# Small triangular matrices turned round through DRAM in wide rows, both chunks and four heads side by side

## The chip, the cores and the metric

The kernel runs on one core of one Trainium2 chip. The metric is device time in microseconds (us). Lower is better.

## The reference

Six residual blocks on x of 1024 tokens by 256 channels: a gated feed-forward with ternary weights, windowed differential attention, the same feed-forward again, a feed-forward whose weights come from a table of 16 values, a gated delta rule, and the table feed-forward again. Only the delta rule bears on this change. It has 16 heads of 128 key and 128 value channels and a state S of 128x128 for each head:

```python
S = S * gt[..., None]
pred = einsum('bhk,bhkv->bhv', kt, S)
delta = (vt - pred) * bt[..., None]
S = S + kt[..., None] * delta[:, :, None, :]
o = einsum('bhk,bhkv->bhv', qt, S)
```

## The kernel before

All matrices are float32. x stays in SBUF, 8 tiles of 128 tokens. The blocks run one after the other; the delta rule (`delta_rule`, L509) takes the span from about 582 to 1706 us.

*The delta rule in chunks.* The 128 tokens of a tile are a chunk; the 16 heads are taken in 4 groups of 4 (HG). Two chunks of one head group are a pair; there are 16 pairs. In a chunk the recurrence becomes a triangular system: keys by keys, decayed, is a strictly lower triangle of 128x128 for each head, and the kernel needs the inverse Z of one plus this triangle, scaled. A pair has 2 chunks x 4 heads = 8 such triangles.

*How Z is made.* The diagonal 16x16 blocks of the triangles are inverted on VectorE (`solve`); the larger blocks are then filled in by matmuls, 16 to 32, 32 to 64, 64 to 128 (`invert`). VectorE wants all 64 diagonal blocks of a pair (8 triangles x 8 blocks) one per partition, with a block's 256 numbers along the partition's row. The matmuls leave the triangles with 64 columns and the row index over the partitions. To get from one layout to the other the data goes through DRAM and back, three times for each pair:

- *dm.* `triangle` (L769) fills the SBUF tile `ml` (128 partitions, 2 chunks, 4 heads, 64 columns) level by level (L850). It is written to the DRAM tile `dm` (L839), one of `[4, 129, 64]` for each chunk. `solve` (L875) reads the 16x16 blocks from there into `xb` (L884), one DMA for each chunk and head, and then multiplies `xb` with `diag` into `nb` (L895), where VectorE's inversion begins (L902 to L933).
- *z.* The inverted blocks `zb` are written block by block to a DRAM array of zeros (L945, one DMA for each chunk and head), and read back as rows (L950, two halves for each chunk).
- *zt.* The same with the transposed blocks `ztb` and full rows of 128 (L945, L947).

The helper `blocks` (L868) gives the 8 diagonal blocks of one triangle in DRAM as a hand-built access pattern: block step 16 x (pitch + 1), row step the pitch, then 16 numbers. The DRAM arrays for z and zt are filled with zeros once, at the start of the delta rule (L605 to L612); there are two sets, used by pairs in turn.

*A neighbour on the same queue.* `prepare` (L661) writes the 8 x 128 scaling coefficients `cf` to DRAM as `cfd` (L684), and `solve` reads them back as `diag` (L879) two pairs later:

```python
cfd = us[0]["cfd"] = dram.tile([2, HG, P], F32, name="cfd", bufs=4)
nc.sync.dma_start(out=cfd.rearrange("c h r -> r c h"), in_=cf)
```

*What sets the order.* Every DMA is issued by the sync engine (SP), in one queue. The pairs overlap: `weave` (L1107) mixes the steps of `prepare` for pair i+2, `triangle` for pair i+1, `solve`, `invert`, `values` and `gates` for pair i, and `advance` and `emit` (the recurrence itself and the output) for pair i-1, by fractions written out at L1141 to L1152. That is the order of the program. The framework then orders each engine's instructions by a simulated timeline (`schedule_with_timeline_sim=True`, L1253) and inserts the semaphore waits. On the chip each engine and the sync queue run strictly in the order so fixed.

Of the kernel before, what the change touches and what calls it, by code (L numbers as in the profile page):

```python
# [10 lines left out]
F32 = mybir.dt.float32  # L11
# [7 lines left out]
P = 128  # L19
# [16 lines left out]
BLK = 16  # L36
HG = 4
NG = NH // HG
NEG = -1e30


# [467 lines left out]
def delta_rule(tc, a, x, xnT, pp, bc, kon, ones, kdw, first):  # L509
# [22 lines left out]
    nc = tc.nc  # L532
# [10 lines left out]
    with ExitStack() as ctx:  # L543
# [49 lines left out]
        small = ctx.enter_context(tc.tile_pool(name="dsm", reuse_waits="tile", bufs=2))  # L593
        blk = ctx.enter_context(tc.tile_pool(name="dblk", reuse_waits="tile", bufs=1))

        turns = []
        for i in range(2):  # L600
            turn = {}
            for nm in ("ml", "mt16", "mt32"):
                turn[nm] = cst.tile([P, 2, HG, 64], F32, name=f"{nm}_{i}")
                nc.gpsimd.memset(turn[nm], 0.0)
            for nm in ("z", "zt"):  # L605
                turn[nm] = dram.tile([2, HG, P, P], F32, name=f"{nm}_{i}", bufs=1)
                for c in range(2):
                    for r in range(2):
                        nc.sync.dma_start(
                            out=turn[nm][c].rearrange("h r s -> r h s")[:, :, 64 * r : 64 * r + 64],  # L610
                            in_=turn["mt16"][:, c],
                        )  # L612
            turns.append(turn)

# [8 lines left out]
        mhalf = cst.tile([P, HG], F32, name="mhalf")  # L623
        nc.gpsimd.memset(mhalf, -0.5)

        lo, hi = slice(0, 64), slice(64, 128)

        parts = [(c, h, half) for c in range(2) for h in range(HG) for half in (lo, hi)]

# [139 lines left out]
        def triangle(us):  # L769

            p = us[0]["p"]
            k, kq, qk, d, turn = p["k"], p["kq"], p["qk"], p["d"], p["turn"]
            kf, d = (t.rearrange("p c h t -> p (c h t)") for t in (k, d))
            full = p["qkf"] = lev.tile([P, 2, HG, P], F32, name="qkf", bufs=3)
            nc.gpsimd.memset(full[hi, :, :, lo], 0.0)
            mt64 = p["mt64"] = lev.tile([64, 2, HG, 64], F32, name="mt64", bufs=2)  # L780
            for i, n in enumerate(LEVELS):
                runs = 64 // n
                rights = lambda ap: ap.rearrange("p b (s two l) -> p b s two l", two=2, l=n)[:, :, :, 1, :]
                if n < 64:
                    pm = pmm.tile([P, 2, 2 * HG, 32], F32, name="pm", tag="pm")
                    for c, h, half in parts:
                        nc.tensor.matmul(  # L787
                            pm[half, :, c * HG + h, :].rearrange("p b (s l) -> p b s l", l=n),
                            lhsT=k[:, c, h, half],
                            rhs=rights(kq[:, :, c, h, half]),  # L790
                            start=True,
                            stop=True,
                        )
                else:

                    pm = pmm.tile([P, 2, 2, HG // 2, 64], F32, name="pm6", tag="pm")
                    for c in range(2):
                        for h in range(HG):
                            nc.tensor.matmul(
                                pm[hi if h % 2 else lo, :, c, h // 2, :],  # L800
                                lhsT=k[:, c, h, lo],
                                rhs=kq[:, :, c, h, hi],
                                start=True,
                                stop=True,
                            )

                dl, dr = (d.rearrange("p (s two) -> p s two", two=2)[:, :, j] for j in range(2))
                kqr = kq.rearrange("p b c h (s two l) -> p b (c h s) two l", two=2, l=n)[:, :, :, 1, :]
                nc.vector.tensor_mul(  # L809
                    kqr,  # L810
                    kqr,
                    dl.unsqueeze(1).unsqueeze(3).to_broadcast([P, 2, 2 * HG * runs, n]),
                )
                kl = left(kf, n)
                nc.gpsimd.tensor_mul(kl, kl, dr.unsqueeze(2).to_broadcast([P, 2 * HG * runs, n]))  # L815
                d2 = lev.tile([P, 2 * HG * runs], F32, name=f"d{i}", bufs=3 if n == 64 else 1)
                nc.gpsimd.tensor_mul(d2, dl, dr)
                d = d2
                if n == 64:
                    for j, half in enumerate((lo, hi)):  # L820
                        nc.scalar.copy(mt64[:, :, j:HG:2, :], pm[half, 0])
                        nc.scalar.copy(full[lo, :, j:HG:2, hi], pm[half, 1])
                    yield
                    continue
                if n == 32:
                    for r0 in (0, 64):
                        at = slice(r0, r0 + 32)
                        nc.scalar.copy(
                            turn["mt32"][at, :, :, 32:64], pm[at, 0].rearrange("p (c h) t -> p c h t", c=2)
                        )  # L830
                        nc.scalar.copy(qk[at, :, 32:64], pm[at, 1])
                    for half in (lo, hi):
                        nc.scalar.copy(full[half, :, :, half], qk[half].rearrange("p (c h) t -> p c h t", c=2))
                    for c, u in enumerate(us):

                        dm = u["dm"] = dram.tile([HG, P + 1, 64], F32, name="dm", bufs=4)
                        for half in (lo, hi):
                            r0 = half.start + half.start // 64
                            nc.sync.dma_start(  # L839
                                out=dm[:, r0 : r0 + 64, :].rearrange("h r s -> r h s"), in_=turn["ml"][half, c]  # L840
                            )
                    yield
                    continue
                mask = kon[:, K_M + i * 32 : K_M + (i + 1) * 32]
                run4 = lambda ap: ap.rearrange("p h (s l) -> p h s l", l=n)
                pred4 = run4(all_heads(mask.bitcast(I32)))
                dst = lambda t: t.rearrange("p h (s two l) -> p h s two l", two=2, l=n)[:, :, :, 1, :]
                flat = lambda t: t.rearrange("p c h t -> p (c h) t")
                if n < BLK:
                    nc.vector.copy_predicated(dst(flat(turn["ml"])), pred4, run4(pm[:, 0]))  # L850
                else:
                    nc.vector.tensor_mul(dst(flat(turn["mt16"])), run4(pm[:, 0]), run4(all_heads(mask)))
                nc.vector.copy_predicated(dst(qk), pred4, run4(pm[:, 1]))
                yield
            p["dall"] = d
            kst = p["kst"] = lev.tile([P, 2, HG, P], F32, name="kst", bufs=2)
            for c, u in enumerate(us):
                if u["n"] < NT - 1:
                    pk = pmm.tile([P, HG, P], F32, name="pk", tag="pm")
                    for h in range(HG):  # L860
                        nc.tensor.transpose(pk[:, h, :], k[:, c, h, :], ident)
                    nc.scalar.copy(kst[:, c], pk)
                u.update(
                    qk=full[:, c], kt=kq[:, 0, c], qt=kq[:, 1, c], kst=kst[:, c], dall=d[:, c * HG : (c + 1) * HG]
                )
                yield

        def blocks(ap):  # L868

            pitch = ap.shape[-1]  # L870
            return bass.AP(
                tensor=ap.tensor, offset=ap.offset, ap=[[BLK * (pitch + 1), P // BLK], [pitch, BLK], [1, BLK]]
            )

        def solve(us, vb):  # L875


# [3 lines left out]
            for c, u in enumerate(us):  # L881
                for h in range(HG):
                    q0 = 32 * c + 8 * h
                    nc.sync.dma_start(  # L884
                        out=xb[q0 : q0 + 8].rearrange("b (i j) -> b i j", j=BLK),
                        in_=blocks(u["dm"][h]),
                    )
            yield
            mat = lambda t: t[:, 0:256].rearrange("p (r c) -> p r c", c=BLK)
# [47 lines left out]
            )  # L937
            z = us[0]["z2"] = lev.tile([P, 2, HG, 64], F32, name="z", bufs=1)
            zt = us[0]["zt2"] = lev.tile([P, 2, HG, P], F32, name="zt", bufs=2)
            for c, u in enumerate(us):  # L940
                for got, to in ((zb, "z"), (ztb, "zt")):
                    full = u["p"]["turn"][to][c]
                    for h in range(HG):
                        q0 = 32 * c + 8 * h
                        nc.sync.dma_start(out=blocks(full[h]), in_=got[q0 : q0 + 8])  # L945
                    if to == "zt":
                        nc.sync.dma_start(out=zt[:, c], in_=full.rearrange("h r s -> r h s"))  # L947
                        continue
                    for r in (slice(0, 64), slice(64, 128)):
                        nc.sync.dma_start(out=z[r, c], in_=full[:, r, r].rearrange("h r s -> r h s"))  # L950
            yield

        def invert(us):
# [303 lines left out]
```

## Time and profile before

| | |
|---|---|
| median of 3 runs | 1788.56 us (1786.34 to 1804.77) |
| the profiled execution | 1780.44 us, its span 1778.7 us |
| mean granted TensorE clock | 0.902 |
| the delta rule, 582 to 1706 us | PE busy 989 of 1124 us |
| its steady part, 770 to 1540 us | PE 706, DVE 579, ACT 478, POOL 328 of 770 us |
| zt read (L947), dm write (L839), z read (L950) | 32, 64, 64 issues of 256, 64, 64 KB |
| xb read (L884), z and zt writes (L945) | 128, 128, 128 issues of 8 KB |
| cfd write, diag read (L684, L879) | 16, 16 issues of 4 KB |

PE is TensorE, DVE VectorE, ACT ScalarE, POOL GpSimd, SP the sync engine; a q after the name is an engine's sequencer, which waits and issues but does not compute. Arrows in the profile point from what is read to what is written: dm<-ml is the DMA that writes dm from ml. In the views of waits a row gives who waited for whom, the total, the number of times and the longest. The packets of a DMA are the runs of bytes that are contiguous on both sides; the profile counts a DMA's semaphore updates as packets too.

### The profile page before, as it was taken

What the parts mean: (1) busy time and instruction counts of PE and PEld (TensorE: products, weight loads), DVE (VectorE), ACT (ScalarE), POOL (GpSimd) and SP (SyncE); (2) the same over time, 40 slices, a digit from 0 to 9 for tenths busy, and PEclk for the clock granted to TensorE, in tenths of its full rate; (3) what the DMA queues carried; (4) which work ended last, traced back from release to release, by engine and by line L of the source; (5) the groups of instructions that cost most, each with busy time, mean ns of one, the idle gap of its engine ahead of it and who ended that gap; (6) DMA issues with size and microseconds to landing.
All of it is one profiled execution on the core that took longest, in us unless ns stands there. A gap on an engine that the chain in (4) does not pass through costs nothing.

```text
span 1778.7 us, 33398 instructions
## 1 busy us (share of the span) xinstructions
PE 1528.3 (86%) x13136; PEld 1105.3 (62%) x13152; DVE 1181.4 (66%) x2567; ACT 879.9 (49%) x2019; POOL 535.5 (30%) x470
## 2 busy tenths in 40 slices
PE   7885868777999766899889889898999998998879
PEld 3433545545455445677767677777777776776745
DVE  3999976574232356767768678786778877877221
ACT  2116273735222344546736646764656674675321
POOL 0022323131001034434533344543434452543100
PEclk9998989889999866798989889999889998989889
DMA  7020000002002001031111121112121120111100
GB/s 243 32 54 26 4 19 1 1 1 66 1 0 44 4 1 30 9 54 28 23 15 40 20 54 28 20 19 46 35 45 24 22 48 9 38 26 20 60 1 24
DMA packets 150349, 54.94 MB, mean 31 GB/s; under 512 B 116784, under 2 KB 142704, under 8 KB 149936
## 3 DMA queue, kind: packets, MB, share of 16 engines
q1 hardware_dynamic: 150192, 52.81, 12.8%
q8 instruction: 104, 1.70, 0.4%
q14 instruction: 53, 0.43, 0.1%
HBM read 39.11 MB, written 11.70 MB: 29 GB/s over the span
## 4 chain that ended last, share of the span: by engine, by line
PE 45%; DVE 22%; ACT 15%; DMA 6%; issue 5%; POOL 3%; SPq 2%; another core or an unknown queue 0%; DVEq 0%; ACTq 0%; POOLq 0%
PE ps L638 6%; PE pg L135 4%; PE po L160 4%; PE pu L135 4%; DMA dm<-ml 4%; PE pm L787 3%; ACT e L319 3%; DVE kq L809 2%; PE pg L697 2%; PE po L365 2%; DVE other L195 2%; PE px L1097 2%; PE pss L675 2%; DVE k L652 2%; PE pr L253 2%
## 5 line engine op out<-in xcount | busy, mean ns | idle before, releaser
L815 POOL TENSOR_TENSOR k<-k,d 128x512 f32<-128x512 f32 x96 | 156.3, 1628 | 299.2 <-PE pm L787 193.3
L787 PE MATMUL pm<-kq,k 128*64 128x64 f32 x3072 | 134.3, 237 | 25.9 <-POOL kq L739 11.0
L787 PEld LDWEIGHTS pm<-kq,k 128*64 128x64 f32 x3072 | 114.6, 148 | 59.1 <-issue 35.7
L809 DVE TENSOR_TENSOR kq<-kq,d 128x1024 f32<-128x1024 f32 x96 | 129.6, 1351 | 23.1 <-remote 8.9
L319 ACT ACTIVATE e<-ps,nm 128x128 f32<-128x128 f32 x256 | 91.5, 397 | 63.6 <-DVE nm L314 62.3
L652 DVE SCALAR_TENSOR_TENSOR k<-ps,pp,k 128x256 f32<-128x256 f32 x192 | 84.9, 475 | 41.7 <-ACT k L650 40.4
L652 DVE SCALAR_TENSOR_TENSOR q<-ps,pp,q 128x256 f32<-128x256 f32 x192 | 86.5, 479 | 24.6 <-ACT q L650 21.7
L652 DVE SCALAR_TENSOR_TENSOR v<-ps,pp,v 128x256 f32<-128x256 f32 x192 | 87.5, 475 | 16.2 <-ACT v L650 14.7
L638 PE MATMUL ps<-xnT,wq 128*128 128x259 f32 x256 | 82.2, 458 | 0.0
L253 PE MATMUL pr<-xnT,wq 128*128 128x512 f32 x128 | 62.9, 625 | 20.8 <-DVE nm L314 9.3
L987 PE MATMUL dz<-zt,mz 64*64 64x32 f32 x1024 | 79.6, 231 | 0.2 <-issue 0.2
L979 PE MATMUL dz<-mz,zt 64*64 64x32 f32 x768 | 73.3, 228 | 7.1 <-ACT mz L972 7.1
L638 PE MATMUL ps<-xnT,wv 128*128 128x259 f32 x256 | 76.5, 425 | 1.2 <-DVE qk L733 0.6
L365 PE MATMUL po<-wo,oT 128*128 128x256 f32 x256 | 64.5, 396 | 14.2 <-ACT oT L362 12.9
L1097 PE MATMUL px<-wdo,oT 128*128 128x256 f32 x256 | 70.8, 422 | 6.6 <-ACT oT L1093 6.4
L650 ACT ACTIVATE q<-ps,pp 128x256 f32<-128x256 f32 x64 | 30.4, 475 | 92.3 <-PE ps L638 92.3
L739 POOL TENSOR_TENSOR kq<-q,ge 128x1024 f32<-128x1024 f32 x16 | 53.5, 3346 | 64.8 <-PE pso L1069 36.6
L987 PEld LDWEIGHTS dz<-zt,mz 64*64 64x64 f32 x1024 | 65.5, 144 | 11.9 <-issue 10.1
L638 PE MATMUL ps<-xnT,wk 128*128 128x259 f32 x256 | 71.6, 417 | 0.5 <-ACT k L650 0.5
L346 POOL TENSOR_TENSOR d<-d,dz 128x512 f32<-128x512 f32 x32 | 34.3, 1072 | 117.3 <-DVE dz L345 86.0
L964 PE MATMUL pmz<-z,mt 64*64 64x64 f32 x1024 | 56.5, 234 | 14.9 <-DMA z<-z 9.9
L964 PEld LDWEIGHTS pmz<-z,mt 64*64 64x64 f32 x1024 | 43.1, 141 | 41.9 <-issue 15.8
(213 smaller groups left out, 3985.9 us busy)
## 6 DMA issues: line engine op xcount, KB each, us to landing
zt<-zt SPq DMA_DIRECT2D x32, 256.0 KB
dm<-ml SPq DMA_DIRECT2D x64, 64.0 KB
z<-z SPq DMA_DIRECT2D x64, 64.0 KB
wq<-in_aWq SPq DMA_DIRECT2D x1, 2048.0 KB
wo<-in_aWo SPq DMA_DIRECT2D x1, 2048.0 KB
wk<-in_dWk SPq DMA_DIRECT2D x4, 512.0 KB
wq<-in_dWq SPq DMA_DIRECT2D x4, 512.0 KB
wv<-in_dWv SPq DMA_DIRECT2D x4, 512.0 KB
```

Source lines behind the costliest of these rows:

```text
L135: nc.tensor.matmul(ps[:n], lhsT=w[:, c, cs], rhs=xnT[:, c, cols], start=(c == 0), stop=(c == KC - 1))
L253: nc.tensor.matmul(pr, lhsT=w[:, c, hcol : hcol + HD], rhs=xnT[:, c, PAD + hf * 512 : PAD + (hf + 1) * 512], start=(c == 0), stop=(c == KC ...
L319: nc.scalar.activation(e[:, s, j, :], ps[:, s, j, :], AF.Exp, bias=nm[:, 4 * s + j : 4 * s + j + 1], scale=SUB**-0.5, accum_out=z[:, s, j ...
L365: nc.tensor.matmul(po, lhsT=oT[:, h, :], rhs=wpool["wo"][:, g * HG + h, :], start=(h == 0), stop=(h == HG - 1),)
L638: nc.tensor.matmul(ps[:, 0 : 2 * P + 3], lhsT=w[nm][:, c, h * HD : (h + 1) * HD], rhs=xnT[:, c, PAD + t0 - 3 : PAD + t0 + 2 * P], start=(c ...
L652: nc.vector.scalar_tensor_tensor(yh, xi, pp[:, col : col + 1], yh, ALU.mult, ALU.add)
L787: nc.tensor.matmul(pm[half, :, c * HG + h, :].rearrange("p b (s l) -> p b s l", l=n), lhsT=k[:, c, h, half], rhs=rights(kq[:, :, c, h, half]),
L809: nc.vector.tensor_mul(kqr, kqr, dl.unsqueeze(1).unsqueeze(3).to_broadcast([P, 2, 2 * HG * runs, n]),)
L815: nc.gpsimd.tensor_mul(kl, kl, dr.unsqueeze(2).to_broadcast([P, 2 * HG * runs, n]))
L964: nc.tensor.matmul(pmz[half, c, h], lhsT=p["turn"][f"mt{n}"][half, c, h], rhs=z[half, c, h], start=True, stop=True,)
L987: nc.tensor.matmul(runs(dz[half, 1, c, h]), lhsT=mz[half, c, h], rhs=right(zt[half, c, h, half], n), start=True, stop=True,)
L1097: nc.tensor.matmul(px, lhsT=oT[:, h, :], rhs=u["w"]["o"][:, h, :], start=(h == 0), stop=(h == HG - 1))
```

## The change

A pair's eight triangles are kept in one flat DRAM array in which a row holds both chunks and all four heads: 2 x 4 x 64 numbers, 2 KB (`ROW` = 512), for dm and z, and 2 x 4 x 128 numbers, 4 KB, for zt. So a row in DRAM has the same order as a partition's row in SBUF. Rows 64 to 127 of dm and z are shifted by 64 numbers (`rows`), so that one step of `blocks` still walks all eight diagonal blocks of a triangle. Its pitch is now the wide row, and triangle i begins at i x width.

```diff
+ROW = 2 * HG * 64
...
+        def rows(ap, half):
+            o = half.start * ROW + half.start
+            return ap[o : o + 64 * ROW].rearrange("(r s) -> r s", s=ROW)
+
+        def blocks(ap, i, width):
+            pitch = 2 * HG * width
+            return bass.AP(
+                tensor=ap.tensor,
+                offset=ap.offset + i * width,
+                ap=[[BLK * (pitch + 1), P // BLK], [pitch, BLK], [1, BLK]],
+            )
...
-                turn[nm] = dram.tile([2, HG, P, P], F32, name=f"{nm}_{i}", bufs=1)
-                for c in range(2):
-                    for r in range(2):
+                wide = ROW if nm == "z" else 2 * ROW
+                turn[nm] = dram.tile([P * wide + 64], F32, name=f"{nm}_{i}", bufs=1)
+                zero = turn["mt16"].rearrange("p c h t -> p (c h t)")
+                if nm == "z":
+                    for half in (lo, hi):
+                        nc.sync.dma_start(out=rows(turn[nm], half), in_=zero[half])
+                else:
+                    for j in range(2):
...
-                    for c, u in enumerate(us):
-                        dm = u["dm"] = dram.tile([HG, P + 1, 64], F32, name="dm", bufs=4)
-                        for half in (lo, hi):
-                            r0 = half.start + half.start // 64
-                            nc.sync.dma_start(
-                                out=dm[:, r0 : r0 + 64, :].rearrange("h r s -> r h s"), in_=turn["ml"][half, c]
-                            )
+                    dm = p["dm"] = dram.tile([P * ROW + 64], F32, name="dm", bufs=2)
+                    for half in (lo, hi):
+                        nc.sync.dma_start(
+                            out=rows(dm, half), in_=turn["ml"][half].rearrange("p c h t -> p (c h t)")
+                        )
...
-                        in_=blocks(u["dm"][h]),
+                        in_=blocks(u["p"]["dm"], c * HG + h, 64),
...
-            for c, u in enumerate(us):
-                for got, to in ((zb, "z"), (ztb, "zt")):
-                    full = u["p"]["turn"][to][c]
-                    for h in range(HG):
-                        q0 = 32 * c + 8 * h
-                        nc.sync.dma_start(out=blocks(full[h]), in_=got[q0 : q0 + 8])
-                    if to == "zt":
-                        nc.sync.dma_start(out=zt[:, c], in_=full.rearrange("h r s -> r h s"))
-                        continue
-                    for r in (slice(0, 64), slice(64, 128)):
-                        nc.sync.dma_start(out=z[r, c], in_=full[:, r, r].rearrange("h r s -> r h s"))
+            turn = us[0]["p"]["turn"]
+            for got, to, width in ((zb, "z", 64), (ztb, "zt", P)):
+                for i in range(2 * HG):
+                    nc.sync.dma_start(out=blocks(turn[to], i, width), in_=got[8 * i : 8 * i + 8])
+                if to == "zt":
+                    nc.sync.dma_start(
+                        out=zt.rearrange("p c h t -> p (c h t)"),
+                        in_=turn[to][0 : 2 * P * ROW].rearrange("(r s) -> r s", s=2 * ROW),
+                    )
+                    continue
+                for half in (lo, hi):
+                    nc.sync.dma_start(out=z[half].rearrange("p c h t -> p (c h t)"), in_=rows(turn[to], half))
```

For each pair the dm writes go from 4 DMAs of 64 KB to 2 of 128 KB, the z reads from 4 to 2, the zt reads from 2 to 1; the 8 block reads of dm and the 16 block writes of z and zt stay, each of 128 runs of 64 bytes. The block writes of z now stand for both chunks ahead of the z reads, then those of zt ahead of the zt read; before, chunk 0's z and zt stood ahead of chunk 1's. The zero fills go from 16 DMAs to 8.

More of the change, by code (lines that the diff above doesn't have):

```diff
@@ L594, in delta_rule @@
         blk = ctx.enter_context(tc.tile_pool(name="dblk", reuse_waits="tile", bufs=1))
+        lo, hi = slice(0, 64), slice(64, 128)
+        def rows(ap, half):
[8 more added lines that the diff above has]
+            )
         turns = []
@@ L605, in delta_rule @@
             for nm in ("z", "zt"):
-                turn[nm] = dram.tile([2, HG, P, P], F32, name=f"{nm}_{i}", bufs=1)
-                for c in range(2):
-                    for r in range(2):
+                wide = ROW if nm == "z" else 2 * ROW
[6 more added lines that the diff above has]
+                    for j in range(2):
                         nc.sync.dma_start(
-                            out=turn[nm][c].rearrange("h r s -> r h s")[:, :, 64 * r : 64 * r + 64],
-                            in_=turn["mt16"][:, c],
+                            out=turn[nm][0 : P * wide].rearrange("(r s) -> r s", s=wide)[:, j * ROW : (j + 1) * ROW],
+                            in_=zero,
                         )
@@ L624, in delta_rule @@
         nc.gpsimd.memset(mhalf, -0.5)
-        lo, hi = slice(0, 64), slice(64, 128)
         parts = [(c, h, half) for c in range(2) for h in range(HG) for half in (lo, hi)]
@@ L866, in triangle @@
                 yield
[L868 to L873, printed above, removed]
         def solve(us, vb):
```

## The prediction

> **What bounds the kernel now.** I read the totals first, then the chain of work that ended last, the waits, and the sync engine's order of time around the lines that the diff edits.
>
> ```profile
> PE 1528.3 (86%) x13136; PEld 1105.3 (62%) x13152; DVE 1181.4 (66%) x2567; ACT 879.9 (49%) x2019; POOL 535.5 (30%) x470
> ...
> DMA packets 150349, 54.94 MB, mean 31 GB/s; under 512 B 116784, under 2 KB 142704, under 8 KB 149936
> ...
> q1 hardware_dynamic: 150192, 52.81, 12.8%
> ```
>
> TensorE is nearest to full; the DMA engines move packets for 12.8% of the span. Bandwidth bounds nothing: only what a late transfer makes others wait for can count. In the steady part of the delta rule (770 to 1540 us) the windows view gives PE 706 busy of 770 us, so all idle time of PE there is 64 us. That caps what any repaired wait can return.
>
> The waits (who waits for whom: us in all, times, longest), first VectorE's and TensorE's within the delta rule (582 to 1706 us), then the sync queue's own:
>
> ```profile
> DVE nb L895 <- DMA xb<-dm: 73.1, 15, 11.1
> ...
> PE pmz L964 <- DMA z<-z: 9.9, 7, 3.6
> ```
>
> ```profile
> SPq L884 <- DMA dm<-ml: 61.6, 19, 9.3
> SPq L950 <- DMA z<-zb: 23.4, 34, 1.7
> SPq L947 <- DMA zt<-ztb: 13.8, 26, 1.7
> ```
>
> The largest wait of VectorE for a transfer is L895: keys by keys go to DRAM (L839, dm) and return as 16x16 blocks (L884, xb). It stands idle 73.1 us over 15 of 16 pairs, and its queue behind L895 stands with it. The chain gives dm<-ml 3.6% of the span, 64 us. So I asked why one landing costs 3 us and another 11. Sync engine's order of time, a clean pair and a bad one, and then the chain in each (start, us, what; a DMA runs here from its issue to its landing):
>
> ```profile
> 713.23 0.38 SPq L684 DMA_DIRECT2D cfd<-cf  x1
> 726.03 2.57 SPq L839 DMA_DIRECT2D dm<-ml  x4
> 728.90 3.70 SPq L884 DMA_DIRECT2D xb<-dm  x8
> ```
>
> ```profile
> 979.13 1.26 SPq L839 DMA_DIRECT2D dm<-ml  x2
> 980.49 0.55 SPq L684 DMA_DIRECT2D cfd<-cf  x1
> 981.09 1.30 SPq L839 DMA_DIRECT2D dm<-ml  x2
> 982.49 11.95 SPq L884 DMA_DIRECT2D xb<-dm  x8
> ```
>
> ```profile
> 727.99 3.24 DMA dm<-ml
> ...
> 732.28 1.55 DMA xb<-dm
> ...
> 981.77 11.24 DMA dm<-ml
> ...
> 994.11 1.61 DMA xb<-dm
> ```
>
> The first fence is the clean pair: cfd went out 12.8 us ahead of dm and is gone. In the second cfd sits between dm's chunks, and the last landing takes 11.24 us. The cause is cfd (L684): 4 KB, but its inner step in DRAM is P, so 1024 packets of 4 bytes. From its issue to the moment the waiting dm clears is 12.5 us here (980.49 to 993.01), and in pairs where cfd went 3 to 8 us ahead of dm the first xb leaves about 11.9 us after it (845.59 to 857.52; 1547.05 to 1558.95), no matter when dm was issued; in two of them 14.8, with a 512 KB weight load queued as well. By that reading 4 pairs of 16 are clean, 8 have cfd shortly ahead, and in 4 (dm at 911, 979, 1232, 1486 us) cfd sits between dm's two chunks; those four stall VectorE 11.1, 10.2, 9.9 and 9.5 us, 40.7 of the 73.1. The change does not touch cfd.
>
> **The skill.** "DMA: Bandwidth & Descriptors", Queues, rings and completion order: the semaphore increment is a strongly ordered write, landing only after every earlier write of that SDMA engine. The trace agrees: all 256 B packets of dm were through by 983.6 in the bad pair, yet it cleared at 993.01, behind cfd's. Same page, Rules for kernel authors: a strided last dim becomes one descriptor per element; that is cfd, 1024 packets of 4 B. Same page, Latency and other measured facts: row pitch in HBM costs from 2 MiB up, 512 KiB does not; the new pitches are 2 and 4 KB, and no run here shows them yet.
>
> **The change part by part.** Sums are made on the profiled execution, 1780.44 us (span 1778.7); the median of the runs shown is 1788.56, 0.5% above, and I scale to it at the end.
>
> *Packets.* Each pair turns its three arrays round once. Per pair the dm writes, z reads and zt reads are 1024 packets each (4x256, 4x256, 2x512) and become 128 each; the fills shrink from 8192 to 768 in all. 150349 - 16x2688 - 7424, less 16 semaphore writes for each of the 88 DMAs fewer, is about 98,500. Directly worth nothing, the engines being 12.8% busy.
>
> *dm.* Four issues of about 0.62 us become two. The nearest row is v<-v (L245, L247), 64 rows of 2 KB, 0.46 to 0.59 us: about 1.15 for two against 2.6. Landing: 3.24 with 256 B packets; a floor is shown by xb (1.55) and z<-z (2.33 in the chain); I take 2.3, range 1.6 to 3.2. Against this, all eight xb now need both halves, where chunk 0's four left early: a longer wait on the sync queue. Behind it stands nothing urgent (after the xb at 982 the next issue is L945 at 1012.43); who waits is L895, and behind that all of VectorE. Clean pair: 0.6 + 2.3 + 0.05 + 2.55 (seven xb issues) + 1.57 = 7.1 us from first dm to nb, against 7.83 (726.03 to 733.86). Gain 0.7; four pairs, 3 us.
>
> *cfd in the middle (four pairs).* cf came ready after the second dm issue, so I take the order dm, dm, cfd, xb. The eight xb then leave early but land behind cfd: cfd at +1.15, clear 12.2 later at 13.35, nb about 1 us after: 14.3 against 16.9 (979.13 to 996.05). Gain 2.6, four pairs: 10 us. Should cfd come between the halves again, the gain is 0; behind xb, about 9 each.
>
> *cfd ahead (eight pairs).* dm clears when cfd does, 11.9 after cfd; xb follows with the same 2.86 + 1.57. Gain 0.
>
> So of 73.1 us some 13 go. What is that on the span? PE itself idles only 15.5 us within these gaps (counted from its instructions), since it works off what was queued, but its clock drops in them (0.77, 0.79, 0.79, 0.85 in the windows of the four bad pairs), and the chain charges dm in full. Between 0.2 (PE idle) and 1 (chain) I take 0.6: 8 us, ends 3 and 13.
>
> *z and zt.* Before, first z write to the last z in SBUF was 12.6 us (1267.56 to about 1280.2), two chunks in turn. After: eight z writes 2.9, landing 1.9, two reads 1.0, landing 2.3: 8.1, or 11 with zt's writes in between. The z reads now wait for eight writes, and any zt write behind them on the sync queue waits too; zt's landing is late for almost nobody today (1.5 us over two waits). Chunk 0's z comes later than now (7.5 us), but L964's 16 matmuls stand in order and want both. Of PE's 9.9 us at L964 I take half: 5 us, range -3 to 10.
>
> *xb reads, z/zt writes.* The same 64 B packets, as many, at a pitch of 2 or 4 KB instead of 256 and 512 B. Bounds: nothing, or, if they became like cfd's 4 B (12 us for 64 per engine), about 0.19 us each: 16 per engine and DMA, 3 us per DMA. I take nothing, on the skill's pitch figure.
>
> *Fills.* 16 issues of 0.55 us at 568 to 577 become 8. SP issues nothing else before 614.50; free, and at most 4 us if that cover were gone.
>
> *Order.* The framework lays out every queue from a simulated timeline (an option at L1253), so a changed transfer can move any instruction. Estimate: plus or minus 10 us, two or three pairs changing kind at 7 us of stall each, times 0.6.
>
> Sum: -8 - 5 = -13: 1767.4 profiled, x 1788.56/1780.44 = 1775.
>
> **Rivals.**
> *B, the stall really goes:* the new order puts cfd behind xb, and every pair is clean. The clean pairs still stall 0 to 5.4 us, mean 3.4; less 0.7, 16 pairs leave 42 of 73 us: 31 x 0.6 + 5 = 24, 1764; with the stall gone entirely 49, 1739. Centre 1757. For it: the cfd that is in the way serves a pair later than the dm behind it, so nothing ties it to that place. Against: cfd is older in the program, and twelve pairs have it ahead or between.
> *C, nothing:* the planner believes xb comes earlier, pulls L895 forward, and VectorE waits for the same cfd; 1788.
> *D, slower, cfd meets dm in more pairs:* each pair that passes from the ahead or clean kind (mean gap 2.7) to the middle kind (10.2) costs 7.5 x 0.6 = 4.5 us. Three such use up the 13; from seven on it is over 1% slower. At ten: 1788.56 - 13 + 45 = 1820. For it: eight pairs are only 3 to 8 us away. Against: two short issues leave less room to fall between.
> *E, serial writes:* the eight blocks' writes now interleave in one array; if the framework saw overlap, each would wait for the one before (0.3 issue, 1.9 landing): eight in 17.6, reads 3.3, z at 20.9 us instead of 12.6, 8 us late in each pair, 16x8x0.6 = 77: 1865. One such wait in each pair (16x1.9x0.6 = 18) already eats the gain. Against: the fills before (two column halves of the same rows, 568.09 to 577) went out back to back.
>
> **How the numbers follow.** About 1% is what a measurement of this kernel can tell from no change. Chances: forecast 0.40 (1775, own range 1760 to 1790), B 0.26, C 0.12, D 0.14, E 0.08. Faster by over 1% (below 1770.7): 0.16 of the forecast, 0.25 of B, 0.01 of C, 0.42. Slower (above 1806.4): D and E but 0.02, 0.01 of the forecast, 0.01 of C, 0.22. Within: 0.36. The range 1745 to 1815 leaves out B's far end (0.05), E and half of D (0.15).
>
> **What would show it.** Packets near 98,500; dm two issues of 0.46 to 0.6 us; landing near 2.3 us where cfd is far; first xb still 11.9 us after a cfd just ahead; the wait at L895's counterpart near 60 us; PE's wait for z below 7. It is wrong if the wait falls under 40 (B), exceeds 80 (D), or z's writes wait for each other (E).

## The result and the profile after

The changed kernel takes 1794.2 us (median of 20 runs, 1787.27 to 1806.39), the kernel before 1786.6 us (median of 20, 1776.15 to 1804.77). The ratio is 1.0047, with a 95% interval of 1.0028 to 1.0067: about 8 us slower, where 13 us faster was forecast. It is within 1%. The profiled execution took 1793.22 us, its span 1791.4 us at a mean clock of 0.902, as before.

The totals and the DMA part of the page of the changed kernel:

```profile
PE 1526.5 (85%) x13152; PEld 1106.9 (62%) x13152; DVE 1186.7 (66%) x2567; ACT 886.2 (49%) x2024; POOL 533.0 (30%) x470
...
DMA packets 98508, 54.41 MB, mean 30 GB/s; under 512 B 74416, under 2 KB 83952, under 8 KB 98096
...
q1 hardware_dynamic: 98352, 52.28, 11.3%
```

The engines do the same work as before. TensorE's busy time is the same within 2 us, so the longer span is idle time of TensorE: 265 us against 250. 52,000 packets are gone, and the time that packets take fell only from 12.8% to 11.3% of the span: what went was not where the time was.

The waits of the changed kernel in the delta rule (582 to 1740 us), VectorE's, then TensorE's, then the sync queue's own (who waited for whom: us in all, times, longest):

```profile
DVE nb L908 <- DMA xb<-dm: 38.8, 11, 7.6
```

```profile
PE pto L1105 <- DVE o L1101: 24.5, 10, 5.3
...
PE pmz L978 <- DMA z<-z: 1.4, 5, 0.4
```

```profile
SPq L897 <- DMA dm<-ml: 55.4, 16, 9.0
...
SPq L958 <- DMA zt<-ztb: 7.5, 18, 0.9
...
SPq L964 <- DMA z<-zb: 5.1, 12, 1.9
```

Everything that the change aims at became shorter. VectorE's wait for the blocks went from 73.1 to 38.8 us, TensorE's for z from 9.9 to 1.4, the sync queue's for z's writes from 23.4 to 5.1. And yet the kernel became slower. The first line of TensorE's list tells where to look: it waits 24.5 us for `o`, the output of the recurrence, which no line of the diff touches. The same row in the kernel before:

```profile
PE pto L1091 <- DVE o L1087: 7.6, 6, 5.3
```

The sync engine's order of time for the two kinds of pair (start, us, what). The pair at 980 had cfd between the halves of dm before; now cfd went 8 us ahead of it. In the second one cfd follows dm, which is left in one pair only:

```profile
972.08 0.39 SPq L707 DMA_DIRECT2D cfd<-cf  x1
980.04 1.11 SPq L859 DMA_DIRECT2D dm<-ml  x2
983.95 2.85 SPq L897 DMA_DIRECT2D xb<-dm  x8
```

```profile
1415.22 1.11 SPq L859 DMA_DIRECT2D dm<-ml  x2
1416.37 0.60 SPq L707 DMA_DIRECT2D cfd<-cf  x1
1418.21 9.12 SPq L897 DMA_DIRECT2D xb<-dm  x8
```

The chain of waits through the second pair:

```profile
1415.73 2.41 DMA dm<-ml
...
1421.42 3.36 SPq L897
...
1427.06 2.44 DMA xb<-dm
```

dm lands in 2.41 us and xb leaves, but one of the eight xb issues then takes 3.36 us on the sync queue where others take 0.3, and the eight spread over 9.1 us: they are stuck behind cfd's 1024 small packets, as the experiment without those packets shows below.

Busy time of the engines from 1285 to 1540 us (window; us, then PE, PEld, DVE, ACT, POOL busy, clock, DMA share, GB/s), the kernel before and the changed one:

```profile
1285.00:1540.00 255.00, 236.98 (x2807) 191.79 (x2808) 197.44 (x395) 162.43 (x266) 109.18 (x96) 0.93 0.16 32
```

```profile
1285.00:1540.00 255.00, 224.93 (x2607) 182.16 (x2605) 184.26 (x368) 157.04 (x256) 104.08 (x92) 0.91 0.12 27
```

In this stretch the changed kernel does 200 matmuls (as the profile counts them) and 12 us of PE work fewer; it had done about as many more than the kernel before by 1285 us, so this is a lead given back. Milestones agree: the inversion (nb) of the pair at 1315.2 us before starts 17 us earlier, at 1298.3; the pair at 1502.1 us before starts at 1500.5; the pair at 1618.4 before starts at 1623.7. The changed kernel is ahead by 17 us, loses 15 of them between 1300 and 1500 us, and falls behind by another 14 us between there and the end.

The order of the instructions is the last piece. If the instruction lists of the two kernels are laid side by side, by operation and tile and with transfers left out, the longest sequence that both share holds 0.88 of VectorE's, 0.88 of ScalarE's, 0.93 of GpSimd's and 0.81 of TensorE's instructions. The planner laid out all four engines anew; VectorE's lists part at 678 us, with the first pair of the delta rule.

### The profile page after: what moved, and what is told of

It reads as the page before. It is cut to its first block, busy times and chain, and to the rows that moved or that the text cites. A ratio compares the mean times of both kernels' runs of the same rounds, so it can differ in the third digit from the quotient of the medians.

```text
span 1791.4 us, 33281 instructions
## 1 busy us (share of the span) xinstructions
PE 1526.5 (85%) x13152; PEld 1106.9 (62%) x13152; DVE 1186.7 (66%) x2567; ACT 886.2 (49%) x2024; POOL 533.0 (30%) x470
## 2 busy tenths in 40 slices
DMA packets 98508, 54.41 MB, mean 30 GB/s; under 512 B 74416, under 2 KB 83952, under 8 KB 98096
## 3 DMA queue, kind: packets, MB, share of 16 engines
q1 hardware_dynamic: 98352, 52.28, 11.3%
## 4 chain that ended last, share of the span: by engine, by line
PE 48%; DVE 20%; ACT 16%; issue 6%; DMA 4%; POOL 4%; SPq 2%; another core or an unknown queue 0%; DVEq 0%; ACTq 0%; POOLq 0%
PE ps L661 7%; PE pm L810 4%; PE po L161 4%; PE pg L136 4%; PE pu L136 4%; ACT e L320 3%; PE px L1111 3%; PE pg L720 2%; DVE other L196 2%; DMA dm<-ml 2%; PE pss L698 2%; PE po L366 2%; DVE kq L832 2%; DVE other L209 2%; PE pr L254 1%
## 5 line engine op out<-in xcount | busy, mean ns | idle before, releaser
L810 PE MATMUL pm<-kq,k 128*64 128x64 f32 x3072 | 142.4, 241 | 33.6 <-POOL kq L762 12.1
L810 PEld LDWEIGHTS pm<-kq,k 128*64 128x64 f32 x3072 | 119.8, 151 | 72.8 <-issue 45.9
L1111 PE MATMUL px<-wdo,oT 128*128 128x256 f32 x256 | 75.7, 447 | 4.1 <-ACT oT L1107 4.1
L366 PE MATMUL po<-wo,oT 128*128 128x256 f32 x256 | 64.6, 396 | 14.1 <-ACT oT L363 12.8
L993 PEld LDWEIGHTS dz<-mz,zt 64*64 64x64 f32 x768 | 57.1, 141 | 16.5 <-issue 7.4
L366 PEld LDWEIGHTS po<-wo,oT 128*128 128x128 f32 x256 | 48.0, 194 | 29.6 <-ACT oT L363 17.7
```

The source lines that it names most:

```text
L366: nc.tensor.matmul(po, lhsT=oT[:, h, :], rhs=wpool["wo"][:, g * HG + h, :], start=(h == 0), stop=(h == HG - 1),)
L810: nc.tensor.matmul(pm[half, :, c * HG + h, :].rearrange("p b (s l) -> p b s l", l=n), lhsT=k[:, c, h, half], rhs=rights(kq[:, :, c, h, half]),
L993: nc.tensor.matmul(runs(dz[half, 0, c, h]), lhsT=zt[half, c, h, half], rhs=left(mz[half, c, h], n), start=True, stop=True,)
L1111: nc.tensor.matmul(px, lhsT=oT[:, h, :], rhs=u["w"]["o"][:, h, :], start=(h == 0), stop=(h == HG - 1))
```

## The experiments

Two things changed together: the transfers, and the order in which four engines do work that the diff never mentions. Theory: the transfers gain a few us and the new order costs more than that. Rival: the new transfers themselves bring little or harm, and the order is innocent. The way to separate them is to pin an order. After the program is traced, this gives each instruction of an engine an edge, without a semaphore, from the one that stood ahead of it in the kernel whose order is wanted; DMA issues on the sync engine stay free:

```python
def pin(tc, nc):
...
    info = mybir.DependencyInfo(mybir.DependencyClass.NoSync, mybir.DependencyReason.DATA)
    for engine, packed in ORDER.items():
...
        for a, b in zip(order, order[1:]):
            tc.add_manual_dep(made[b], made[a].name, info, reason="pinned order")
```

In the traces of the pinned runs VectorE, ScalarE and GpSimd run exactly the sequence that they were pinned to, TensorE too but for records missing from the traces (and but for the one move of the tail experiment).

"Old order" is the order of the kernel before, "new order" that of the changed kernel. Ratios are to the kernel before on the same chip, with 95% intervals. The runs were spread over several chips, and a ratio carries over only roughly: the same kernel, with wide rows and cfd in rows (below), gave 0.9626 on one chip and 0.9544 on another. So differences under about 1% are read only between runs of one chip.

### Transfers and order, crossed

*wide_old_order*: the changed kernel, and `pin(tc, nc)` with the old order of PE, DVE, ACT and POOL.

> The changed transfers, with the four compute engines held in exactly the order of instructions of the kernel before. Theory 1 (the transfers themselves help, and the new order of instructions gives it back and more): faster than before by 8 to 15 us, ratio 0.991 to 0.996, VectorE's wait for xb near 60 us. Theory 2 (the wide transfers are themselves no gain or a loss, since the z reads and the xb reads now wait for both chunks): ratio 1.000 to 1.008, with PE's waits for z grown.

*narrow_new_order*: the kernel before, and `pin(tc, nc)` with the changed kernel's order.

> The old transfers, with the four compute engines held in exactly the order of instructions of the changed kernel. Theory 1: slower than the changed kernel, ratio to the kernel before 1.008 to 1.015, with the 7 us of feed-forward matmuls in front of the last chunk's recurrence in the tail as in the changed kernel. Theory 2: 0.995 to 1.000, since the loss came with the transfers and goes with them.

*dm_wide_old_order*: the kernel before with the diff's dm alone (writes and xb reads), old order.

```diff
...
-                            nc.sync.dma_start(
-                                out=dm[:, r0 : r0 + 64, :].rearrange("h r s -> r h s"), in_=turn["ml"][half, c]
-                            )
+                        nc.sync.dma_start(
+                            out=rows(dm, half), in_=turn["ml"][half].rearrange("p c h t -> p (c h t)")
+                        )
...
-                        in_=blocks(u["dm"][h]),
+                        in_=wide_blocks(u["p"]["dm"], c * HG + h, 64),
```

> Only dm in wide rows (two writes of 128 KB, all eight block reads from it), z and zt as before, the four compute engines held in the old order. Theory 1: most of the gain of the transfers is here, ratio 0.993 to 0.997, VectorE's wait for xb 60 us. Theory 2: 0.999 to 1.003.

*z_wide_old_order*: the kernel before with the diff's z and zt alone, old order; of dm nothing:

```diff
-                        in_=blocks(u["dm"][h]),
+                        in_=old_blocks(u["dm"][h]),
```

> Only z and zt in wide rows, dm as before, the four compute engines held in the old order. Theory 1: ratio 0.996 to 0.999, PE's wait for z below 7 us where it was 9.9. Theory 2: 1.000 to 1.006, chunk 0's matmuls now waiting for chunk 1's blocks.

Measured:

| | old order | new order |
|---|---|---|
| old transfers | 1 | 1.0227 (1.0193 to 1.0261) |
| wide transfers | 0.9978 (0.9963 to 0.9993) | 1.0047 (1.0028 to 1.0067) |
| dm alone wide | 1.0000 (0.9984 to 1.0016) | |
| z and zt alone wide | 1.0045 (1.0028 to 1.0062) | |

The old-order column and the 1.0227 are of one chip. The changed kernel's 1.0047 is its first measurement, repeated on another chip at 1.0043; its differences from the other cells are rough.

In the order of the kernel before, the transfers make it faster by 0.2%, 4 us, less than theory 1 wanted and not the loss of theory 2. The old transfers in the new order lie beyond theory 1's 1.015. The new order by itself costs 2.3% with the old transfers, on one chip; with the new ones about 0.7%, across chips. By the same rough reckoning the transfers are worth 1.8% in the new order. The waits show why the two don't add. First *wide_old_order*, VectorE's and TensorE's, then *narrow_new_order*, the same two:

```profile
DVE nb L908 <- DMA xb<-dm: 68.7, 13, 9.0
```

```profile
PE pmz L978 <- DMA z<-z: 13.3, 5, 5.5
```

```profile
DVE nb L895 <- DMA xb<-dm: 45.4, 13, 10.7
```

```profile
PE pmz L964 <- DMA z<-z: 26.2, 18, 4.1
```

The new order puts the matmuls on z so early that the old, slower z makes TensorE wait 26.2 us over 18 waits; it counts on the faster z. And it needs no wide dm to cut VectorE's wait: with the old transfers the row is 45.4 us already, against 73.1. So of the 34 us that the row lost in the changed kernel, the transfers gave 4 in the old order and 7 in the new, and the order the other 28 or 30. Even those 4 are doubtful. With dm alone wide, in the old order, the row is longer than the 73.1 of the kernel before, where theory 1 had 60:

```profile
DVE nb L907 <- DMA xb<-dm: 80.2, 14, 10.4
```

The rival falls as far as it denies the order a part; it holds in that the transfers bring little.

z and zt alone cost 0.45% here. That number lies in theory 2's range, but its reason doesn't show: TensorE's wait for z was 9.1 us, not more than the 9.9 before. Nor do the parts add up: dm alone brings 0, z and zt alone cost 8 us, both together bring 4. The order of the DMA issues wasn't pinned; whether it did this stays open.

### Is any new order worth that much?

*placebo_plan*: the kernel before, with one lane of the program's interleaving shifted by a hundredth. No transfer and no instruction changes.

```diff
-                lanes.append((0.55, 0.7, 7, values(now)))
+                lanes.append((0.56, 0.71, 7, values(now)))
```

> The kernel before with nothing changed but one fraction of the interleaving: the values lane from 0.55 to 0.70 becomes 0.56 to 0.71. No transfer and no instruction differs; the planner lays the engines out anew, about as differently as the change did. It measures how far a new order alone moves the time. Theory (orders scatter by about 1%): off the kernel before by 0.5 to 1.5%, either way. Rival (orders are of equal worth, within 0.3%): 0.997 to 1.003.

It took 1.0335 (1.0306 to 1.0363): 60 us for nothing but another order, with the row of VectorE at 60.8 us, below the 73.1 of the kernel before. A shift that means nothing moves this kernel by more than either the change or its forecast. One such shift gives one draw and no distribution, but it shows that 12 us from a new order need no cause in the transfers. Both expectations fall: theory had at most 1.5%. The new order was a little further from that of the kernel before than the changed kernel's is (0.86 of VectorE's and 0.77 of TensorE's instructions in the longest shared sequence).

### What in the new order costs

*wide_new_order_tail*: the changed kernel in its own order, but eight matmuls of the last feed-forward (pg and pu, two records each in the profile) moved behind the last state update and its readers (pn and pso). The chain of waits of the changed kernel shows them ahead of pn:

```profile
1674.76 0.89 PE pw L1062 x8
1675.66 1.72 PE pg L136 x4
1677.38 1.72 PE pu L136 x4
1679.09 1.72 PE pg L136 x4
1680.81 1.72 PE pu L136 x4
1682.53 0.89 PE pn L1069 x8
```

6.9 us of work that nobody waits for stands ahead of the state update, the output `o` and all that follows from it; afterwards TensorE idles twice for 5.3 us at `pto` for `o`, once more than in the kernel before.

> The changed kernel, its compute engines held in its own order but for one move on TensorE: eight gate and up matmuls of the last feed-forward, which stand ahead of the state update of the second last chunk but one, go behind that chunk's output matmuls, where the old order has them. Theory (the new order loses 5 to 7 us there): 5 to 7 us below the changed kernel, ratio to the kernel before about 1.001, and PE's 5.3 us of idle ahead of the next transpose of o filled. Rival (the tail is bounded by the chain over GpSimd and ScalarE, and the matmuls only fill it): no difference to the changed kernel, 1.004 to 1.006.

With the matmuls moved the chain has pn right behind the state's weights:

```profile
1659.57 0.91 PE pw L1062 x8
1660.48 0.02 issue
1660.50 0.59 ACT wt L1064
1661.10 0.04 issue
1661.14 1.16 PE pn L1069 x8
```

It took 0.9971 (0.9953 to 0.9988), and from the last nb to the end 160.8 us instead of 167.7. One of the two idle times of 5.3 us is gone. That ratio was against another chip's kernel before, so both were run again on one chip: the changed kernel (*changed_same_chip*) and the moved tail (*wide_new_order_tail_again*).

> The changed kernel as it is, timed anew beside the kernel before, as a measure for the version with the moved matmuls (0.9971), which ran on a chip where the kernel before took 1781 us. Theory (the move is worth its 5 to 7 us and the rest of the 0.76% between the two ratios is the chip): 0.999 to 1.003. Rival (the move is worth the whole 13 us): 1.003 to 1.007.

> The changed kernel with the eight matmuls moved, beside the one above on the same chip. Theory: 5 to 7 us, 0.3 to 0.4%, below it. Rival: 13 us, 0.7% or more.

1.0043 (1.0025 to 1.0061) and 0.9997 (0.9983 to 1.0010). The move is worth 0.46%, 8 us, somewhat more than the theory's 7 and well under the rival's 13. So eight matmuls in the wrong place are as much as the whole measured loss. The same kernel gave 0.9971 on one chip and 0.9997 on the other; the rest of the 0.76% is the chip.

### What holds up dm

The prediction said that cfd's 1024 packets of 4 B, not dm's size, set the landing. *wide_cfd_rows_old_order*: the changed kernel, old order, with cfd written as rows of 32 B; the turn to blocks is made by the read of diag two pairs later, now eight DMAs, 4 B packets there.

```diff
-            cfd = us[0]["cfd"] = dram.tile([2, HG, P], F32, name="cfd", bufs=4)
-            nc.sync.dma_start(out=cfd.rearrange("c h r -> r c h"), in_=cf)
+            cfd = us[0]["cfd"] = dram.tile([P, 2 * HG], F32, name="cfd", bufs=4)
+            nc.sync.dma_start(out=cfd, in_=cf.rearrange("p c h -> p (c h)"))
...
-            nc.sync.dma_start(out=diag, in_=us[0]["cfd"].rearrange("c h (b i) -> (c h b) i", i=BLK))
+            turned = us[0]["cfd"].rearrange("(b i) q -> q b i", i=BLK)
+            for q in range(2 * HG):
+                nc.sync.dma_start(out=diag[8 * q : 8 * q + 8], in_=turned[q])
```

> Wide transfers in the old order of the compute engines, and cfd written in rows of 32 bytes (128 packets in place of 1024 of 4 bytes); the 4-byte packets move to the read of diag, eight DMAs. Theory (the slow writes of cfd bound most landings of dm): first xb leaves 2 to 3 us after dm in every pair but those with a weight load, VectorE's wait for xb from 68.7 to below 40 us, ratio 0.985 to 0.993. Rival (any 4-byte packets are as slow, or the wait for xb is covered by PE's queue): the wait stays above 55 us or the ratio stays at 0.996 to 1.000.

It took 0.9626 (0.9598 to 0.9654). VectorE's wait and the sync engine's order of time in the pair that has cfd right behind dm:

```profile
DVE nb L910 <- DMA xb<-dm: 19.6, 10, 4.6
```

```profile
956.15 1.14 SPq L859 DMA_DIRECT2D dm<-ml  x2
957.38 0.54 SPq L707 DMA_DIRECT2D cfd<-cf  x1
959.15 2.86 SPq L899 DMA_DIRECT2D xb<-dm  x8
```

The same sequence as at 1415 us above, and the eight xb go out in 2.86 us instead of 9.12. The first xb leaves 1.8 to 1.9 us after the second dm issue in every pair but two, which have a weight load ahead in the queue (3.5 and 5.0 us). The wait falls by 49 us against *wide_old_order*, the time by 3.5%, some 63 us, more than twice what the theory had; by the same kernel's ratio on the chip of the last group, 0.9544, it is 4.3%, some 78 us.

The 4-byte packets are still there, as reads, and the rival's "any 4-byte packets are as slow" can be settled from the landings in the trace. Here no read of diag is issued within 13 us ahead of a dm, so the early xb says nothing of it. But each of the 128 reads of 128 packets landed 2.0 to 4.1 us after its issue, median 2.1. The write of 1024 packets took 8.3 to 12.0 us in the kernel before, median 10.6 (to the last semaphore update that its trace has); in rows of 32 bytes it took 1.4. So these reads aren't as slow. One read of 1024 packets wasn't run.

*wide_cfd_rows*: the same without `pin`, the planner free.

> The changed kernel with cfd written in rows of 32 bytes, the planner free to order it. Theory (cfd bounds the landings): VectorE's wait for xb from 38.8 to below 25 us; the time is that gain plus what the new order gives or takes, 0.985 to 1.005. Rival (cfd is covered): wait as in the changed kernel, 38 us.

0.9789 (0.9763 to 0.9814), with the wait at 21.6 us. The rival falls. In the trace the planner's order is again that of the changed kernel, on all four engines. It is 1.7%, 30 us, dearer than the old order on the same chip, with the wait nearly the same. With the 2.3% of *narrow_new_order* this is the second price of the new order taken on one chip.

*narrow_cfd_rows_old_order*: the kernel before with cfd in rows, old order.

> The old, narrow transfers and the old order of the compute engines, with cfd written in rows of 32 bytes and diag read by eight DMAs of 4-byte packets. It tells what the wide rows are worth once cfd is out of their way. Theory 1 (they shorten the way to xb and to z, 2 to 5 us for each pair, and it counts now): 0.968 to 0.975, slower than the wide kernel with the same cfd (0.9626). Theory 2 (cfd was everything): 0.960 to 0.966, as the wide one.

0.9581 (0.9556 to 0.9605), on another chip than the wide one. Theory 1 falls: with cfd cured the wide rows show no gain. For anything finer the two had to be set side by side.

### Are the wide rows worth anything?

Four kernels on one chip, all in the old order, all with cfd in rows: no transfer of the change (*cfd_rows_narrow*), all of them (*cfd_rows_wide*), dm alone (*cfd_rows_dm_wide*), z and zt alone (*cfd_rows_z_wide*). The edits are those shown above.

> Narrow dm, narrow z and zt, cfd in rows, old order: the reference of this group. 0.957 to 0.961.

> Wide dm, wide z and zt. Theory 1 (the wide transfers are worth nothing or cost up to 0.5%, because both chunks' block reads and matmuls wait for the later chunk, which takes the place of the shorter landing): equal to the narrow one or up to 8 us slower. Theory 2 (the difference seen was the chip): 3 to 8 us faster than the narrow one.

> Wide dm alone. Theory 1: within 3 us of the narrow one, since first dm to nb goes from 7.9 to 7.5 us only. Theory 2: 3 to 5 us faster.

> Wide z and zt alone. Theory 1: 4 to 8 us slower than the narrow one, as it was with the slow cfd (1.0045), because chunk 0's z is there later. Theory 2: 0 to 4 us faster, all of z being there 4 us earlier.

| | median, us | ratio |
|---|---|---|
| narrow | 1719.01 | 0.9572 (0.9545 to 0.9599) |
| all wide | 1712.34 | 0.9544 (0.9523 to 0.9566) |
| dm alone wide | 1718.32 | 0.9578 (0.9555 to 0.9601) |
| z and zt alone wide | 1716.34 | 0.9569 (0.9546 to 0.9593) |

All wide is 6.7 us below narrow by the medians, with four and five runs, but the intervals overlap, as all four do: no gain of the wide rows is shown here. It agrees in size with the 4 us of *wide_old_order*. That narrow would be as fast or faster, as the two runs on different chips suggested, isn't borne out. The loss of z and zt alone didn't come back, so it isn't theirs in general; what caused it in that one kernel stays open. The fastest version is the changed transfers with cfd in rows and the old order, 4.6% under the kernel before here and 3.7% on another chip.

## Why the prediction was wrong

The forecast was faster by 13 us; the kernel is slower by 8. The range, 1745 to 1815, holds 1794. The step that failed is *Order*, the new layout of the engines, which was put at zero give or take 10 us; the gain that it ate, 13 us, was itself sized too high, at about 4 instead. By the prediction's own steps:

*Packets*: about 98,500 forecast, 98,508 counted. That this is worth nothing directly held.

*dm*: two issues in 1.15 us, 1.11 measured; landing 2.3 us, 2.41 measured. The clean pair was put at 7.1 us from dm to nb. In the old order the four clean pairs took 8.4 on average, against 8.0 before; in the new order such pairs took 7.5 to 8.2. Only with cfd in rows did half of the pairs come to 7.1 to 7.7. The issues and the landing were right, but the path to nb was not shorter by them.

*cfd in the middle*: the order dm, dm, cfd, xb came about as written, with cfd at +1.2. In *wide_old_order*, which has such pairs at the four places named, dm to nb took 15.3, 15.7, 15.1 and 14.5 us, mean 15.2, where 14.3 was forecast and 16.9 stood before: 1.7 us a pair instead of 2.6. The xb issues behind cfd are themselves held up: the last goes out 11.1 to 11.6 us after cfd and still has to land. In the changed kernel all four moved away from this kind and one other pair came into it.

*cfd ahead*: "dm clears when cfd does, 11.9 after cfd". In the changed kernel nine pairs have cfd 4.8 to 8.5 us ahead of dm, and where no weight load was near the first xb mostly left 11.9 to 12.2 us after cfd, at most 14.2 (at 980, with cfd 8.0 us ahead of dm, xb left at 983.95: 11.9). No gain from a shorter dm there, as forecast. It rests on what the Trainium skill, "DMA: Bandwidth & Descriptors", Queues, rings and completion order, says of the semaphore's write, which lands after every earlier write of its DMA engine. *wide_cfd_rows_old_order* bears out that cfd's writes are what is waited for: without the 4 B writes the first xb comes 1.8 us after dm.

*The 13 us of stall*, first failed size: in the order that the prediction reasoned in, VectorE's wait fell by 4.4 us (73.1 to 68.7), not by 13, and with dm alone wide it rose to 80.2. The four middle pairs gave 7 us instead of 10, the 3 us of the clean ones did not come, and the eight pairs with cfd ahead took 12.2 us from dm to nb instead of 11.3. In sum the way from dm to nb was no shorter: 192 us over the 16 pairs, 190 before. The pairs with cfd ahead took 12.4 with the old dm too (*z_wide_old_order*), so their loss isn't shown to be the wide rows'.

*What a us of stall is worth*: 0.6 was taken. Removing 49 us by cfd in rows gave 63 to 78 us. That is 1.3 to 1.6, above even the chain's 1. The two profiles show where the excess lies. The span fell by 69 us (1784.4 to 1715.2), but TensorE's idle time by only 29; the other 40 are its busy time, 1522.0 to 1481.8 us for the same matmuls, at a mean clock of 0.927 instead of 0.906. The prediction saw that the clock drops in the gaps, but let it go into the 0.6. The factor erred low, which would have made the forecast worse, not better.

*z and zt*, second failed size: of TensorE's 9.9 us at L964 half was to go. In the old order it did not: 9.1 us with z and zt alone wide, 13.3 with everything wide, over fewer, longer waits (5 instead of 7, longest 5.5). One thing that fits is that the first read of z lands later, 7.2 us after the first z write instead of 5.4 (medians of the 16 pairs); the step named that and then put it aside because the matmuls "want both". In the new order the wait fell to 1.4 us. That took both: the same order waits 26.2 us with the old z, and the old order 13.3 with the new one. That z's writes go out back to back (rival E excluded) and z arrives earlier was right: all of it was there 7.9 us after the first z write in the changed kernel, median, against 12.2; 8.1 was forecast. One reading was wrong: 1267.56, from which the step counts 12.6 us, is the first write of zt; z's own stands at 1269.04, and from it the pair took 10.7.

*Order*, the step that decided: "plus or minus 10 us, two or three pairs changing kind at 7 us of stall each, times 0.6". It was added as a spread with mean zero and priced only as far as pairs change kind with respect to cfd. That part went well, by luck: one middle pair instead of four, and the wait at 38.8 us, under the 40 at which rival B would hold, yet not the time that B gave. But a new order also moves TensorE's work, and that wasn't priced. The eight matmuls ahead of the last state update cost 8 us, and between 1285 and 1540 us PE did 12 us less work. The new order costs 41 us with the old transfers and 30 us with the wide ones and cfd in rows, each on one chip; about 12 us with the wide transfers alone, across chips (1.0047 less 0.9978, of 1789). The placebo's order costs 60. So the spread should have been some 10 to 60 us, against a direct gain of 4. No run here tells how orders fall on average, so zero as the middle isn't refuted in general; it failed for this order.

*Rival D* got the sign but not the cause: cfd meets dm in fewer pairs, not more. *C*, that nothing changes, has the cause of the small direct gain, cfd, right. Its number, 1788, lay nearest.

What stays open: which misplacements cost the 12 us between 1300 and 1500 us (only the tail's 8 us was isolated, by moving it); why z alone cost 0.45% in one kernel; and why the clock is higher with cfd in rows.

## What to carry to other kernels

Before you make a late transfer smaller, look at what stands ahead of it in the same queue: here one 4 KB write of 1024 packets in each pair cost some 75 us in all with the narrow rows and 63 to 78, by the chip, with the wide ones, where the wide rows themselves gave 4 to 7 at most. Where a planner lays out the engines, an edit to a DMA is two edits; compare in a pinned order before you judge the edit, and try a shift that means nothing to see how much an order alone can move. Set kernels that differ by less than 1% side by side on one chip. A shorter total of one wait isn't a gain until the span says so: here the wait that was aimed at was nearly halved while the kernel got slower.

## What the runs showed of the hardware

- A write of 1024 packets of 4 B to DRAM (cfd) landed 8.3 to 12.0 us after its issue in the kernel before, and held up for some 12 us what came behind it. The same 4 KB in rows of 32 B landed in 1.4 us (median). Reads of 128 packets of 4 B (diag, eight for a pair) landed in 2.1 us. The Trainium skill, "DMA: Bandwidth & Descriptors", Rules for kernel authors, warns of one descriptor per element without telling reads and writes apart.
- DMA issues behind such a write are held up on the sync queue itself: one xb issue took 3.36 us (2.75 in *wide_old_order*) where 0.3 is usual. With the same sequence and cfd in rows the longest took 0.33.
- Blocks of 64 B read at a pitch of 2 KB instead of 256 B cost nothing that shows: the eight xb of a pair went out in 2.85 us, as in the kernel before. The pitch figure of the Trainium skill, "DMA: Bandwidth & Descriptors", Latency and other measured facts, on which the prediction leant, starts at 512 KiB; at 2 KB it is the trace that shows it.
- The granted clock was higher with cfd in rows: on the chip of the last group 0.901 before and 0.924 to 0.931 in the four kernels (medians of their runs). What raises it isn't shown.
